# Graph attention with a residual layer norm: seven own blocks for the tile of five to seven keys, one list of edges, and paired small steps in layer norm

## The chip, the core and the metric

The kernel runs on one NeuronCore of a Trainium2 chip. TensorE (PE) multiplies matrices, VectorE (DVE) and ScalarE (ACT) work element by element, GpSimd (POOL) issues the indirect DMAs and computes a few powers, SyncE (SP) issues most plain DMAs. Each engine takes its instructions in the order in which the program wrote them, and waits on semaphores for the others. The metric is the device time of one execution in microseconds (us).

## The reference

`x` is 16 batches of 1024 nodes with 512 features, all in float32. `adj` is a 1024 x 1024 matrix of zeros and ones that all batches share; its chance of a one falls with the row and the column number, so that most nodes have few neighbours and a few have many. There are 8 heads of 64 features.

```python
q = (x @ Wq + bq).reshape(b, n, H, HD)      # k and v likewise
scores = jnp.einsum('bqhd,bkhd->bhqk', q, k) / jnp.sqrt(jnp.float32(HD))
scores = scores + (1.0 - adj)[None, None, :, :] * -1000000000.0
attn = jax.nn.softmax(scores, axis=-1)
out = jnp.einsum('bhqk,bkhd->bqhd', attn, v).reshape(b, n, d)
x = layernorm(x + out @ Wo + bo)            # mean and variance over the 512 features, eps 1e-5
```

A query without any neighbour gives every key the same weight, so its attention is the mean of all values.

## The kernel before

**Tiles and blocks.** The kernel doesn't multiply dense score matrices. It sorts the 1024 nodes by their number of keys (their neighbours) and cuts them into eight tiles of 128 queries: tile 0 has the queries with the fewest keys, tile 7 those with the most. A *block* is 128 pairs of a query and one of its keys. For each block the rows of k and v are gathered from DRAM by an indirect DMA into the tile `kvg` (L1292). There are two kinds of blocks:

- An *own* block of a tile has one key for each of the tile's 128 queries, in the order of the tile. Its queries are the rows of the tile `qt`, loaded once for all own blocks of the tile. A query with fewer keys than the tile has own blocks leaves its place empty: the gather skips it, and a large negative bias takes its weight to zero.
- A *deep* block packs the keys that are left over, of any of the tile's queries. Its queries have to be gathered as well (`qg`, L1246), and its result has to be brought back to the tile's order by a matrix of zeros and ones in `sums`.

`OWN` has the number of own blocks of each tile, `BLOCKS` that of deep blocks, `DEGREE` the length of the list of a query's left-over keys. Before, tile 6 (five to seven keys) had five own blocks and a deep one, and tile 7 seven and five. Tile 1 (one key each) is not computed in blocks at all, and tile 0 is computed for two batches at once from batch 2 on; so a batch has 34 blocks or 32, and the 16 batches have 530.

**What a block costs.** Each block passes these steps: product of q and k on VectorE (`products`, L1313), sum over each head's 64 features on VectorE (`scores`, L1317), exponential on ScalarE (`exponentials`, L1328), and weighing of v by it (`weigh`). The function `by_act` says which engine weighs: own blocks after the first of their tile always go to ScalarE, as eight instructions of one head each (L1341). The first block of a tile and the deep ones go to ScalarE or, as one instruction, to VectorE (L1345), by whether a number is even:

```python
if 0 < i < OWN[t]:
    return True
turn_of = b + i if b and i else n
return n < total - NBT and (turn_of % 2 == 0 or n < NBT // 2)
```

Here `b` is the batch, `i` the block's number in its tile and `n` its number in the whole program. `add_own` adds an own block (but the first) to the tile's first on VectorE (L1357); `add_up` adds a deep block by two products with `sums` on TensorE, which together have four matrix instructions in the trace (L1366, L1367). `normalise` closes a tile: where it had deep blocks, two VectorE instructions add what TensorE has summed (L1378 and L1379), and then each head is divided by its sum.

**Lists of edges.** For a tile with deep blocks `edges(t)` builds the list of left-over keys before they are used: it gathers the tile's rows of `adj`, finds the keys with repeated maxima over 1024 numbers (L646, L665, L667), and places them with small matrix products (L682, L707, L728). `REST_FROM` has the iteration in which each list starts: tile 7 at -24, tile 6 at -6. `ranks` writes the own keys into `key_row` and `absent`, and `lookups` turns each row of keys into places, by one small indirect DMA each.

**The dense part.** `pair`, `transpose_x` and `product` put the work of every batch on TensorE: transposing x, the products with the weights for q, k and v (k and v by a scheme with seven products instead of eight), and the product with `Wo` (`finish`). Until 12 blocks before the last batch starts there is such work ahead in the list `fronts`; after that, only the product with `Wo` is left, some of it from tiles that were spilled to DRAM (`SPILL`).

**The order.** A Python loop writes the whole program, one iteration for each block; it has `n` as its counter. In iteration n it writes the gathers up to block n + 8, the exponential of block n + 3, the product and the sum of block n + 4, the weighing on VectorE of block n + 1 or on ScalarE of block n + 2, and the addition of block n. The function `later(k, ...)` puts an instruction k iterations on, and `later_last` puts it at the end of that iteration. TensorE gets as much dense work in each iteration as `share` and the block's own load allow (`paced`).

**Layer norm.** `complete` adds the residual to a tile (in `Y`, six buffers), and then come a row sum with it on VectorE (L1113), the sum of squares on ScalarE (L1120, `spread`), `variance` on VectorE (L1123), `power` on GpSimd (L1126; L1174 for two tiles), `shift` on VectorE (L1129), `norm_out` on ScalarE (L1134) and the store (L1148). While there is work in `fronts` each tile does all of these by itself (`single`). After that two tiles share the power, and still have a variance and a shift each. `load_y` loads the residual into a buffer of `Y`; it is only called while fewer than five buffers are held.

Of the kernel before, what the change touches and what calls it, by code (L numbers as in the profile page):

```python
# [14 lines left out]
OP = mybir.AluOpType  # L15
# [3 lines left out]
EPS = 1e-5  # L19
# [4 lines left out]

OWN = (2, 1, 2, 3, 4, 5, 5, 7)
BLOCKS = (0, 0, 0, 0, 0, 0, 1, 5)
DEGREE = (8, 8, 8, 8, 8, 8, 16, 80)

AHEAD = 8
KG_BUFS, Q_BUFS, QT_BUFS, PV_BUFS, Y_BUFS = 8, 5, 3, 5, 6
# [29 lines left out]
MORE_RANKS_AT = 1  # L62
NORMS_AT = 18
LOOK_FROM = -17
REST_FROM = {7: -24, 6: -6}

PRODUCT = 0.86
SUM = 0.87
# [6 lines left out]
P = 128  # L75
# [103 lines left out]
def kernel(  # L179
# [36 lines left out]
    nc = tc.nc  # L216
    B, N, D = x.shape
# [5 lines left out]
    scale = 1.0 / HD ** 0.5  # L223
    assert N == 1024 and D == 512 and HD == 64 and max(BLOCKS) <= NT
    NS = sum(BLOCKS)
    NB = NS + sum(OWN)
    first = [sum(BLOCKS[:t]) for t in range(NT)]
    SHORT = [t for t in range(NT) if not BLOCKS[t]]
    SHORT_KEYS = max(OWN[t] for t in SHORT)
    assert SHORT == list(range(len(SHORT))) and max(OWN) <= TOP  # L230
    own = [SHORT_KEYS * t for t in SHORT]
    for t in range(len(SHORT), NT):
        own.append(own[-1] + (OWN[t - 1] if t > len(SHORT) else SHORT_KEYS))
    NK = own[-1] + OWN[-1]
    NBT = NB - OWN[ONE_KEY]
    assert OWN[ONE_KEY] == 1 and BLOCKS[ONE_KEY] == 0

# [17 lines left out]
    with ExitStack() as main:  # L255
# [18 lines left out]
        nc.gpsimd.iota(place, pattern=[[1, SPAN]], base=1, channel_multiplier=0, allow_small_or_imprecise_dtypes=True)  # L274
        placed = one.tile([P, max(BLOCKS)], F32, name="placed")
        nc.gpsimd.iota(placed, pattern=[[P, max(BLOCKS)]], base=1, channel_multiplier=1, allow_small_or_imprecise_dtypes=True)
# [171 lines left out]
        def later(k, fn):  # L448
            plan.setdefault(now[0] + k, []).append(fn)

        def later_last(k, fn):
            rest.setdefault(now[0] + k, []).append(fn)
# [554 lines left out]
        loaded, half, wide = {}, [], []  # L1007
# [89 lines left out]
        def complete(b, t, p, plain):  # L1097
            n, rows, offset = rows_of(b, t)
            y, p = Y[b, t][0:n, :], p[0:n, :]
            ending = not fronts and now[0] >= total - 1  # L1100
            single = fronts or ending or n < P
            if single:
                st = small.tile([P, 5], F32, name="stats", bufs=6)[0:n, :]
            else:

                second = bool(half)
                if not second:
                    half.append([small.tile([P, 2, 5], F32, name="stats_2", bufs=5)])
                st2 = half[0][0]
                st = st2[:, int(second), :]  # L1110
            if plain:
                nc.vector.tensor_tensor(y, p, y, op=OP.add)
            nc.vector.scalar_tensor_tensor(  # L1113
                y, bo_bc[0:n, :] if plain else p, 1.0, y, op0=OP.mult, op1=OP.add, accum_out=st[:, 0:1]
            )

            def spread():

                sq = work.tile([P, D], F32, tag="ysq", name=f"ysq_{b}_{t}", bufs=1)
                nc.scalar.activation(sq[0:n, :], y, AF.Square, bias=st[:, 0:1], scale=-float(D), accum_out=st[:, 2:3])  # L1120

            def variance():
                nc.vector.tensor_scalar(st[:, 2:3], st[:, 2:3], 1.0 / D ** 3, EPS, op0=OP.mult, op1=OP.add)  # L1123

            def power():
                nc.gpsimd.tensor_tensor(st[:, 3:4], st[:, 2:3], neg_half[0:n, :], op=OP.pow)  # L1126

            def shift():
                nc.vector.scalar_tensor_tensor(  # L1129
                    st[:, 4:5], st[:, 0:1], -1.0 / D, st[:, 3:4], op0=OP.mult, op1=OP.mult  # L1130
                )

            def norm_out():
                nc.scalar.activation(y, y, AF.Identity, bias=st[:, 4:5], scale=st[:, 3:4])  # L1134
                if not fronts and now[0] >= total:
                    later_last(1, store)
                else:
                    later(2, store)

            def centre():  # L1140
                nc.vector.tensor_scalar(st[:, 4:5], st[:, 0:1], 1.0 / D, None, op0=OP.mult)

            def last_norm_out():
                nc.vector.tensor_scalar(y, y, st[:, 4:5], st[:, 3:4], op0=OP.subtract, op1=OP.mult)
                store()

            def store():
                nc.gpsimd.indirect_dma_start(  # L1148
                    out=out_rows[b, t], out_offset=bass.IndirectOffsetOnAxis(ap=rows, axis=0),
                    in_=y, in_offset=None, element_offset=offset,  # L1150
                )
                del Y[b, t]

            later_last(0 if ending else 1, spread)
            if ending and (b, t) == closes[total - 1]:
                for step in (centre, variance, power, last_norm_out):
                    later(1, step)
            elif ending:
                later(1, variance)
                later(1, power)  # L1160
                later_last(1, shift)
                later_last(1, norm_out)
            elif single:
                late = 1 if fronts else 0
                later(2 + late, variance)
                later(3 + late, power)
                later(4 + 2 * late, shift)
                later_last(5 + 2 * late, norm_out)
            elif second:
                later(3, variance)  # L1170
                mate_shift, mate_norm_out = half.pop()[1]

                def powers():
                    nc.gpsimd.tensor_tensor(  # L1174
                        st2[:, :, 3:4], st2[:, :, 2:3], neg_half[:, :, None].to_broadcast([P, 2, 1]), op=OP.pow
                    )

                def shifts():
                    mate_shift()
                    shift()  # L1180

                later(4, powers)
                shift_at = 6 if fronts else min(6, max(5, total - now[0]))
                later(shift_at, shifts)
                later_last(shift_at, mate_norm_out)
                later_last(7 if shift_at == 6 else 5, norm_out)
            else:
                later(3, variance)
                mine = half[0]
                mine.append((shift, norm_out))  # L1190

                def alone():
                    if half and half[0] is mine:
                        half.pop()
                        power()
                        later(2, shift)
                        later_last(3, norm_out)

                later(6, alone)

# [281 lines left out]
        done, coming, spilled, gathered, fronts, guarded = [], [], [], [0], [], []  # L1484
# [31 lines left out]
        with tc.manual_schedule():  # L1516
# [20 lines left out]
            n = -LEAD_IN  # L1537
# [120 lines left out]
```

## Time and profile before

| | |
|---|---|
| time, median of 3 runs | 1847.21 us (1845.62 to 1847.8) |
| span of the profiled execution | 1840.4 us |
| median less span | 6.8 us |
| busy, share of the span | PE 98%, DVE 92%, ACT 85%, POOL 66% |
| instructions in the span | 25352 |
| granted TensorE clock, mean | 0.996 |

The profile has one execution, and its own time outside the span is not stated; the median of the runs stands 6.8 us over the span, and differences in the span are carried to the median one for one. "Busy" counts an instruction from its start to its end. Instructions of one engine overlap a little, so what one more of them costs its engine is read from start to start in the timeline, not from its duration. The page that sums up the profile gives, for each group of instructions, the line, the engine, the tiles, the number of instructions after an x, the time busy and the mean of one in ns, and after a bar the idle time ahead of it with what ended it.

### The profile page before, as it was taken

The numbers are of one execution on the slowest core, as the hardware profiler recorded it, in microseconds if no ns is written. First come the engines' busy times: TensorE is split into PE (matmuls) and PEld (weight loads), VectorE is DVE, ScalarE is ACT, GpSimd is POOL, SyncE is SP. The second block draws the span as 40 slices with busy tenths as digits, with TensorE's granted clock in tenths as the row PEclk, the third lists the DMA queues.
The fourth block names the chain that finished last, engine by engine and source line by source line (L and its number), as shares of the span: only waits on it lengthen the run. The fifth ranks groups of instructions, "written<-read, shape, count | busy, mean of one in ns | idle before, by whom it ended". The sixth has DMA issues, their size and how long they took to land.

```text
span 1840.4 us, 25352 instructions
## 1 busy us (share of the span) xinstructions
PE 1798.2 (98%) x5140; PEld 876.2 (48%) x5140; DVE 1693.7 (92%) x3473; ACT 1563.2 (85%) x6183; POOL 1215.3 (66%) x1142
## 2 busy tenths in 40 slices
PE   7999999999999999999999999999999999999997
PEld 3444454554444454444444445444544444444443
DVE  6889889999989999999999999999999999997986
ACT  3637869989889898999889988989799999987886
POOL 1367766766565776767757666677666767665786
PEclk9999999999999999999999999999999999999998
DMA  7358787989889899999988998999989999889995
GB/s 287 106 190 253 256 325 237 346 301 327 308 280 314 295 336 319 344 316 308 347 316 310 346 335 276 343 321 322 339 315 325 314 355 326 306 324 325 338 319 191
DMA packets 198791, 558.54 MB, mean 303 GB/s; under 512 B 33450, under 2 KB 33470, under 8 KB 198626
## 3 DMA queue, kind: packets, MB, share of 16 engines
q0 software_dynamic: 112640, 370.50, 59.3%
q1 hardware_dynamic: 82910, 180.52, 26.2%
q10 hardware_dynamic: 3076, 5.82, 0.9%
q14 instruction: 122, 1.00, 0.2%
q8 instruction: 43, 0.70, 0.2%
HBM read 420.30 MB, written 157.45 MB: 314 GB/s over the span
## 4 chain that ended last, share of the span: by engine, by line
PE 69%; DVE 10%; ACT 9%; DMA 4%; issue 3%; POOL 1%; SPq 0%; POOLq 0%; DVEq 0%; ACTq 0%
PE po L799 17%; PE pq L799 15%; PE pp L956 12%; PE z L956 9%; PE x L956 9%; ACT pv L1341 5%; DVE qk L1313 2%; PE poT L1401 2%; PE pxT L757 2%; PE sum L1367 2%; DVE s L1317 2%; PE sum L1366 2%; DVE pv L1357 1%; ACT sq_k L809 1%; DMA kvg<-kv_pair,place_row 1%
## 5 line engine op out<-in xcount | busy, mean ns | idle before, releaser
L1341 ACT ACTIVATE pv<-kvg,pv 128x64 f32<-128x64 f32 x3600 | 907.5, 341 | 0.0
L1292 POOL DMA_INDIRECT kvg<-kv_pair,place_row x462 | 526.7, 1140 | 307.4 <-ACT pv L1341 99.6
L799 PE MATMUL pq<-wq,xT 128*128 128x512 f32 x792 | 367.8, 596 | 0.0
L1317 DVE TENSOR_REDUCE s<-qk 128x8 f32<-128x512 f32 x530 | 360.7, 681 | 6.8
L799 PE MATMUL po<-wo,oT 128*128 128x512 f32 x792 | 359.3, 594 | 0.7 <-ACT oT L1405 0.7
L1313 DVE TENSOR_TENSOR qk<-qt,kvg 128x512 f32<-128x512 f32 x434 | 297.2, 685 | 1.1 <-DMA kvg<-kv_rows,key_row 0.6
L956 PE MATMUL x<-b,xT 128*128 128x512 f32 x504 | 237.3, 593 | 0.5 <-ACT e L969 0.4
L956 PE MATMUL pp<-t,s 128*128 128x512 f32 x504 | 237.0, 593 | 0.0
L1357 DVE TENSOR_TENSOR pv<-pv,pv 128x520 f32<-128x520 f32 x329 | 228.3, 694 | 4.3 <-ACT pv L1341 4.2
L799 PEld LDWEIGHTS po<-wo,oT 128*128 128x128 f32 x792 | 149.1, 191 | 170.0 <-issue 160.2
L799 PEld LDWEIGHTS pq<-wq,xT 128*128 128x128 f32 x792 | 148.4, 192 | 161.9 <-issue 149.9
L1010 POOL DMA_INDIRECT x<-in_x_dram,asked_row x120 | 133.0, 1108 | 77.8 <-issue 21.3
L1148 POOL DMA_INDIRECT out_dram<-y,asked_row x129 | 146.9, 1139 | 39.1 <-issue 21.2
L1328 ACT ACTIVATE pv<-s,absent 128x8 f32<-128x8 f32 x434 | 127.0, 294 | 44.0 <-DVE s L1317 40.8
L809 ACT ACTIVATE sq_k<-kv 128x128 bf16<-128x128 f32 x512 | 150.8, 301 | 6.4 <-DVE kv L979 3.4
L956 PEld LDWEIGHTS pp<-t,s 128*128 128x128 f32 x504 | 94.7, 191 | 108.1 <-issue 99.4
L956 PEld LDWEIGHTS x<-b,xT 128*128 128x128 f32 x504 | 94.2, 191 | 107.4 <-issue 99.0
L956 PE MATMUL z<-b,s 128*128 128x512 f32 x252 | 119.2, 596 | 7.0 <-DVE kv L984 7.0
L1246 POOL DMA_INDIRECT qg<-q_rows,query_row x96 | 104.4, 1088 | 28.4 <-issue 26.9
L956 PE MATMUL z<-t,s 128*128 128x512 f32 x252 | 118.6, 593 | 0.0
L956 PE MATMUL pp<-t,xT 128*128 128x512 f32 x252 | 118.5, 593 | 0.0
L1134 ACT ACTIVATE y<-y,stats 128x512 f32<-128x512 f32 (+1 forms) x128 | 102.7, 806 | 17.0 <-DVE stats L1129 17.0
(279 smaller groups left out, 2713.0 us busy)
## 6 DMA issues: line engine op xcount, KB each, us to landing
kv_pair<-kv SPq DMA_DIRECT2D x98, 512.0 KB
q_rows<-q SPq DMA_DIRECT2D x106, 256.0 KB
qt<-q_rows SPq DMA_DIRECT2D x98, 256.0 KB
residual<-x SPq DMA_DIRECT2D x83, 256.0 KB
y<-residual SPq DMA_DIRECT2D x83, 256.0 KB
kv_rows<-kv SPq DMA_DIRECT2D x15, 512.0 KB
kvg<-kv_pair,place_row POOLq DMA_INDIRECT x462, 6.9
kv_pair<-kv SPq DMA_DIRECT2D x28, 256.0 KB
```

The source lines that it names most:

```text
L799: nc.tensor.matmul(p, lhs(c), w[:, c, :], start=(c == 0), stop=(c == NPAIR - 1))
L809: nc.scalar.activation(sq, s[:, ts(h, P)], AF.Square, scale=scale, accum_out=sums[:, h:h + 1])
L956: nc.tensor.matmul(R[bank], l[:, ts(c, P)], right[:, c, :], start=(first and c == 0), stop=(c == 1), skip_group_check=True,)
L1010: nc.gpsimd.indirect_dma_start(out=y, out_offset=None, in_=x_rows, in_offset=bass.IndirectOffsetOnAxis(ap=asked_row[:, t:t + 1], axis=0), ...
L1148: nc.gpsimd.indirect_dma_start(out=out_rows[b, t], out_offset=bass.IndirectOffsetOnAxis(ap=rows, axis=0), in_=y, in_offset=None, element_o ...
L1246: nc.gpsimd.indirect_dma_start(out=q, out_offset=None, in_=q_rows[b % ROWS], in_offset=bass.IndirectOffsetOnAxis(ap=rows, axis=0))
L1292: nc.gpsimd.indirect_dma_start(out=KG[n], out_offset=None, in_=rows, in_offset=bass.IndirectOffsetOnAxis(ap=(place_row if b else key_row)[ ...
L1313: nc.vector.tensor_tensor(QK[n], q, KG[n][:, 0:D], op=OP.mult)
L1317: nc.vector.tensor_reduce(S[n], QK.pop(n).rearrange("p (h d) -> p h d", d=HD), axis=AX.X, op=OP.add)
L1328: nc.scalar.activation(PV[n][:, D:], S.pop(n), AF.Exp, bias=bias)
L1341: nc.scalar.activation(pv[:, ts(h, HD)], v[:, ds(D + h * HD, HD)], AF.Copy, scale=pv[:, D + h:D + h + 1])
L1357: nc.vector.tensor_tensor(PV[b, t], PV[b, t], pv, op=OP.add)
```

## The change

Tile 6 gets seven own blocks and no deep one. `SHORT`, the tiles without deep blocks, is then tiles 0 to 6, and the only list of edges that is left is that of tile 7. A batch has 35 blocks or 33, and the program 546, of which 80 are deep where 96 were. Before, tile 6 was the last of each batch from batch 2 on; now its blocks stand ahead of those of tile 7, and tile 7 is the last.

In layer norm the tiles go in pairs also while there is work in `fronts`. A pair has one `variances`, one `powers` and one `shifts`, each for two numbers a row. A tile that finds no second one within nine iterations (five where `fronts` is empty) does the steps alone.

```diff
-OWN = (2, 1, 2, 3, 4, 5, 5, 7)
-BLOCKS = (0, 0, 0, 0, 0, 0, 1, 5)
-DEGREE = (8, 8, 8, 8, 8, 8, 16, 80)
+OWN = (2, 1, 2, 3, 4, 5, 7, 7)
+BLOCKS = (0, 0, 0, 0, 0, 0, 0, 5)
+DEGREE = (8, 8, 8, 8, 8, 8, 8, 80)
...
-REST_FROM = {7: -24, 6: -6}
+REST_FROM = {7: -24}
...
-            single = fronts or ending or n < P
+            single = ending or n < P
...
             elif second:
-                later(3, variance)
-                mate_shift, mate_norm_out = half.pop()[1]
+                mate_norm_out = half.pop()[1]
+
+                def variances():
+                    nc.vector.tensor_scalar(
+                        st2[:, :, 2:3], st2[:, :, 2:3], 1.0 / D ** 3, EPS, op0=OP.mult, op1=OP.add
+                    )
...
                 def shifts():
-                    mate_shift()
-                    shift()
-
+                    nc.vector.scalar_tensor_tensor(
+                        st2[:, :, 4:5], st2[:, :, 0:1], -1.0 / D, st2[:, :, 3:4], op0=OP.mult, op1=OP.mult
+                    )
+
+                later(3, variances)
                 later(4, powers)
                 shift_at = 6 if fronts else min(6, max(5, total - now[0]))
                 later(shift_at, shifts)
                 later_last(shift_at, mate_norm_out)
                 later_last(7 if shift_at == 6 else 5, norm_out)
             else:
-                later(3, variance)
                 mine = half[0]
-                mine.append((shift, norm_out))
+                mine.append(norm_out)
 
                 def alone():
                     if half and half[0] is mine:
                         half.pop()
-                        power()
-                        later(2, shift)
-                        later_last(3, norm_out)
-
-                later(6, alone)
+                        variance()
+                        later(1, power)
+                        later(3, shift)
+                        later_last(4, norm_out)
+
+                later(9 if fronts else 5, alone)
```

## The prediction

> **What bounds the kernel now.** I read the page of the whole span first, then the busy time of each engine in stretches, since a share over the span mixes stages.
>
> ```profile
> span 1840.4 us, 25352 instructions
> ...
> PE 1798.2 (98%) x5140; PEld 876.2 (48%) x5140; DVE 1693.7 (92%) x3473; ACT 1563.2 (85%) x6183; POOL 1215.3 (66%) x1142
> ```
>
> TensorE is busy for nearly the whole span, with VectorE six points behind. The stretches (start and end in us, then length, and busy PE, PEld, DVE, ACT and POOL) show where that holds:
>
> ```profile
> 110.00:300.00 190.00, 184.87 (x534) 88.92 (x534) 167.78 (x367) 139.93 (x577) 135.32 (x127) 1.00 0.79 265
> 300.00:400.00 100.00, 100.00 (x295) 50.06 (x294) 96.72 (x193) 92.38 (x382) 73.21 (x71) 1.00 0.91 324
> 400.00:600.00 200.00, 197.62 (x563) 96.31 (x563) 181.72 (x361) 174.87 (x704) 127.42 (x122) 1.00 0.87 298
> 600.00:700.00 100.00, 100.00 (x290) 49.17 (x290) 97.53 (x194) 90.60 (x360) 74.42 (x67) 1.00 0.93 325
> 700.00:1000.00 300.00, 299.48 (x867) 146.46 (x866) 286.64 (x556) 272.72 (x1127) 199.45 (x179) 1.00 0.92 321
> 1000.00:1100.00 100.00, 96.99 (x283) 47.87 (x282) 96.72 (x186) 89.59 (x364) 68.71 (x65) 1.00 0.96 336
> 1100.00:1200.00 100.00, 100.00 (x295) 49.49 (x294) 94.44 (x186) 91.80 (x379) 62.73 (x58) 1.00 0.89 309
> 1200.00:1300.00 100.00, 99.95 (x289) 49.17 (x288) 97.65 (x193) 94.12 (x381) 72.60 (x65) 1.00 0.92 332
> 1300.00:1400.00 100.00, 99.29 (x293) 49.22 (x292) 95.00 (x183) 89.90 (x375) 66.83 (x61) 1.00 0.91 322
> 1400.00:1500.00 100.00, 99.61 (x289) 48.96 (x287) 97.43 (x193) 93.16 (x368) 70.37 (x66) 1.00 0.92 324
> 1500.00:1600.00 100.00, 95.44 (x278) 46.87 (x277) 98.42 (x190) 94.18 (x403) 65.44 (x60) 1.00 0.94 333
> 1600.00:1841.00 241.00, 225.61 (x620) 107.23 (x618) 199.96 (x494) 188.78 (x648) 166.02 (x157) 0.98 0.83 296
> 1000.00:1025.00 25.00, 25.00 (x74) 12.36 (x73) 24.68 (x51) 23.94 (x99) 17.65 (x18) 1.00 0.94 331
> 1525.00:1550.00 25.00, 22.38 (x63) 10.95 (x62) 24.72 (x47) 23.43 (x95) 18.48 (x18) 1.00 1.00 371
> ```
>
> From 300 to 1400 TensorE hardly pauses and sets the pace. But VectorE has only two to five points of room in most of these stretches, and in 1500:1600 the order is turned round: VectorE at 98.42, TensorE down to 95.44. So two engines share the bound, and the change takes from one of them and gives to the other.
>
> **The deep block, on TensorE.** These rows are the timeline of TensorE (start, length), the two products of one deep block and what follows:
>
> ```profile
> 908.65 0.59 PE L1366 MATMUL sum<-pv,sums 128*128 128x256 f32 x2
> 909.08 0.61 PE L1367 MATMUL sum<-pv,sums 128*128 128x264 f32 x2
> 909.53 1.02 PE L956 MATMUL z<-b,s 128*128 128x512 f32 x2
> ```
>
> From start to start they take 909.53 - 908.65 = 0.88 us. (The durations, 380 and 387 ns a piece, would make 1.53; they overlap, so I take the spacing.) One such block in each of 16 batches goes: 14.1 us.
>
> **The blocks, on VectorE.** The timeline of VectorE, read from start to start in the same way:
>
> ```profile
> 1203.94 0.15 DVE L1378 TENSOR_TENSOR rden<-sum,pv 128x8 f32<-128x8 f32 x1
> 1204.01 0.68 DVE L1379 TENSOR_TENSOR o<-sum,pv 128x512 f32<-128x512 f32 x1
> 1204.61 0.19 DVE L1383 RECIPROCAL rden<-rden 128x8 f32<-128x8 f32 x1
> ...
> 1207.62 0.68 DVE L1313 TENSOR_TENSOR qk<-qt,kvg 128x512 f32<-128x512 f32 x1
> 1208.22 0.69 DVE L1357 TENSOR_TENSOR pv<-pv,pv 128x520 f32<-128x520 f32 x1
> 1208.83 0.68 DVE L1317 TENSOR_REDUCE s<-qk 128x8 f32<-128x512 f32 x1
> 1209.42 0.15 DVE L1129 SCALAR_TENSOR_TENSOR stats<-stats 128x1 f32<-128x1 f32 x1
> 1209.49 0.69 DVE L863 TENSOR_TENSOR vsum<-vsum,kv 128x512 f32<-128x512 f32 x1
> ```
>
> Product 0.60, addition 0.61, sum over heads 0.59, a small step 0.07. A batch gains two own blocks: 2 x 1.80 = +3.60. It loses a deep one: product and sum, -1.19, and L1378 and L1379 in the closing of tile 6, -0.67. That leaves +1.74.
>
> **Who weighs** is less visible. By the rule in `by_act` the first block of a tile goes by whether its number in the program is even. Before, batches have 34 or 32 blocks, so every batch starts at an even number, and in a batch of 34 the first blocks of its tiles stand at 0, 2, 5, 9, 14, 20 and 28: two of seven odd. After, batches have 35 or 33 and every second one starts at an odd number; there the first blocks stand at 0, 2, 4, 8, 13, 19 and 27 from an odd start, which makes four of seven odd. In the other batches (33 blocks) they stand at 0, 2, 6, 11, 17 and 25 from an even start: three odd, where the positions 0, 2, 6, 11, 18 and 26 before had one. With the deep blocks (by b + i) VectorE weighs 6 blocks in every batch from 2 to 14, where it weighed 5 and 4 by turns. Counted over all blocks that is 99 where there were 80.
>
> ```profile
> L1341 ACT ACTIVATE pv<-kvg,pv 128x64 f32<-128x64 f32 x3600 | 907.5, 341 | 0.0
> L1345 DVE TENSOR_TENSOR pv<-kvg,pv 128x512 f32<-128x512 f32 x80 | 54.9, 686 | 0.0
> L1328 ACT ACTIVATE pv<-s,absent 128x8 f32<-128x8 f32 x434 | 127.0, 294 | 44.0 <-DVE s L1317 40.8 <-DVE stats L1123 2.7
> ```
>
> The count of 80 is there. So VectorE has 1.5 more a batch, +0.90 at the 0.60 of like shapes. ScalarE weighs 546 - 99 = 447 blocks for 3600 / 8 = 450: -6 us at 907.5 / 450 = 2.02 each. It has 16 exponentials more, +5. ScalarE stays where it is, and the two extra own blocks of each batch fall on VectorE in the end.
>
> **Layer norm.** The rows before: 97 single powers and 16 for two.
>
> ```profile
> L1126 POOL TENSOR_TENSOR stats<-stats,neg_half 128x1 f32<-128x1 f32 (+1 forms) x97 | 67.2, 693 | 20.7 <-DVE stats L1123 18.9
> ...
> 300.00:1600.00 1300.00, 62.16 (x77) 1.00 0.91 320
> ACT y L1134 <- DVE stats L1129: 17.0, 12, 3.5
> SPq L1035 <- DMA out_dram<-y,asked_row: 36.1, 7, 15.5
> ```
>
> The second row is L1134 alone: 77 tiles are normed between 300 and 1600. Less seven half tiles that stay single and a few without a mate, some 33 pairs each save a variance and a shift: 33 x 2 x 0.07 = 4.6 us, 0.36 a batch. The powers saved lie beside other work on GpSimd, 66% busy. The costs: in a pair the first tile's L1134 now stands in the iteration of the shift, not one later, so ScalarE may wait for VectorE; this is the 17.0 us above, 12 times, all of it after 1700 where pairs exist now. At 17.0 / 16 pairs, 33 pairs would wait 35 us. Queued behind it on ScalarE are the exponential and the weighing of later blocks, which VectorE needs. I cost it at nothing: ScalarE is idle 1300 - 1183 = 117 us from 300 to 1600 (the stretches above). Without that cover it is 35. The first tile of a pair also holds its buffer of `Y` some five iterations longer. SP waits for such a buffer for 36.1 us after 1600 and, in the view of SP's waits, not once between 150 and 1600; behind it stand the stores of q and of k and v. I take nothing here too; if it came here as it does after 1600, it would be some 36.
>
> **Gathers.** 16 more of k and v and 16 fewer of q leave GpSimd's count of issues alone, and no row of k and v is added, as empty places are skipped.
>
> **The list of tile 6.**
>
> ```profile
> L665 DVE MAX8 kl<-codes 128x8 f32<-128x1024 f32 x2 | 2.4, 1217 | 0.0
> PE z L956 <- DVE kv L984: 1.1, 1, 1.1
> ```
>
> Two maxima of 1.2 us over 1024 numbers, two more passes over as many and a dozen small steps leave VectorE. TensorE loses only what waited: 1.1 us between 110 and 150 (second row), and about 0.5 of small products. I take -1.6; the bounds are 0 and TensorE's whole idle time in 110:300, 5.1.
>
> **The sum, stretch by stretch.** Sums over heads (L1317) count the blocks:
>
> ```profile
> 110.00:300.00 190.00, 30.30 (x45) 1.00 0.79 265
> 300.00:1600.00 1300.00, 288.90 (x425) 1.00 0.91 320
> 1600.00:1841.00 241.00, 41.48 (x61) 0.98 0.83 296
> ```
>
> At 530 / 16 = 33.1 to a batch that is 1.36, 12.8 and 1.84 batches, so nearly one in each 100 us between 300 and 1600. There TensorE loses 0.88 per 100 us, and VectorE gains 1.74 + 0.90 - 0.36 = 2.28. A stretch then takes the longer of two times: TensorE's new busy time with the idle time that it has now, or VectorE's new busy time divided by the share that it can reach. That share is the unknown: 0.984 was reached over 100 us (1500:1600), 0.987 to 0.989 over 25 us (the last two rows of the stretches), 0.9695 over 1300 to 1600 ((95.00 + 97.43 + 98.42) / 300). I take 0.984, from the only stretch in which VectorE plainly led:
>
> - 300: (96.72 + 2.28) / 0.984 = 100.6, so +0.6; in the same way 600: +1.4, 1000: +0.6, 1200: +1.6, 1400: +1.3, 1500: +2.3. Sum +7.8.
> - 400 to 600 stays TensorE's: -1.8; 1100 and 1300 too: -0.9 each. 700 to 1000: VectorE has 293.5 / 0.984 = 298.3, so -1.7. Sum -5.3.
>
> That is +2.5 from 300 to 1600. Elsewhere TensorE leads: 1.36 x 0.88 = -1.2 and -1.6 for the list before 300, 1.84 x 0.88 = -1.6 after 1600. Total -1.9 on a span of 1840.4; taken off the median of 1847.2 (6.8 above the span), about 1845. At 0.988 the stretches give -0.9 and the time is 1842, and at 0.980 they give +6.5 and 1849. In own blocks the addition stands between the product and the sum that needs it, as in the rows above, which should fill VectorE a little better than deep blocks do; so I take **1844**.
>
> The Trainium skill speaks against the change here. Its page "Perfetto Trace Analysis", section "Identifying the Most-Contended Engine", says that matmul busy time is no good measure for TensorE, that its weight loads are (48% here), and that occupancy is fair for VectorE. VectorE with 92% would then be the engine to relieve, and the sum would be its growth alone, 1876 (the last rival), in place of 1844. The trace agrees in 1500:1600 and not in 300:400, where TensorE has no gap.
>
> **The rivals.**
>
> - *TensorE keeps the end throughout.* VectorE reaches 0.99 and more and its extra work fits: -0.88 x 12.8 - 4.4 = -15.7, so 1831.5. For it: 1000:1025, with TensorE at 25.00 and VectorE at 24.68. Against: 1525:1550, where VectorE at 24.72 left TensorE at 22.38.
> - *VectorE takes over and can't be filled better than over 1300 to 1600*, 0.9695. Each stretch with VectorE over 95% now then grows: 300 +2.1, 600 +2.9, 700 to 1000 +2.7, 1000 +2.1, 1200 +3.1, 1400 +2.8, 1500 +3.9, less 1.7 in the others: +17.9, with -4.4 outside +13.5, so **1861**, slower. It decides from a share of about 0.98 downward. For it: the dense work comes to VectorE in lumps. Against: the share rose in the stretches when there was more to do.
> - *The pairs bring waits*: of the 35 us on ScalarE a third reaches VectorE, 1844 + 12 = 1856. Against it is ScalarE's 117 us of idle time.
> - *VectorE bounds all of the span as it is.* Then its growth, 12.8 x 2.28 = 29, is added in full: 1876. Against it: in 1100:1200 VectorE has 94.44 and TensorE no gap at all. The rule of the Trainium skill named above would have it so.
>
> **How the numbers follow.** Forecast 0.45 (its own range 1840 to 1850), TensorE throughout 0.27, VectorE at the lower share 0.17, waits by pairs 0.06, VectorE everywhere 0.05. A measurement of this kernel tells about 0.2%, 3.7 us, from no change. Faster by more: 0.27 and a good third of the forecast, 0.43. Slower: most of the last three, 0.25. The rest, 0.32, is within. The range of 1830 to 1858 leaves out the far ends of the first and the slower rivals.
>
> **What would show it.** After, L1366 and L1367 should have 160 each, L1345 99 and L1341 3576, and powers for two should be near 50. VectorE should stand at 97 to 98.5% in most stretches from 300 to 1600, with TensorE at 97 to 99. TensorE above 99% throughout would speak for the first rival, VectorE at 97 or less with TensorE at 97 or less for the second, and L1134 waiting for L1129 before 1600 for the third. The prediction is wrong if VectorE's busy sum doesn't rise by 20 to 35 us.

## The result and the profile after

The changed kernel takes 1878.27 us (1873.15 to 1879.64) where the kernel before takes 1847.21: 1.016 times as long, interval 1.0146 to 1.0174. That is slower, 34 us over the forecast of 1844 and 20 over the end of the range.

The page of the changed kernel: span and busy time.

```profile
span 1877.9 us, 25037 instructions
...
PE 1803.6 (96%) x5071; PEld 864.8 (46%) x5071; DVE 1717.2 (91%) x3387; ACT 1566.2 (83%) x6174; POOL 1216.1 (65%) x1102
```

VectorE has 23.5 us more to do than before and ScalarE 3.0. TensorE is the surprise: on each of the two lines of a deep block it has 160 instructions where it had 192, some 14 us less in all, yet its busy time *rose* by 5.4 us. Its idle time, span less busy, went from 42.2 us to 74.3. So the 37.5 us of span are 32.1 of new idle time on TensorE and 5.4 of longer busy time.

Groups of the changed kernel (line, operation, count, then busy us and mean ns); each form came in the number that the prediction gives, or near it:

```profile
L1323 DVE TENSOR_REDUCE s<-qk 128x8 f32<-128x512 f32 x546 | 371.1, 680 | 6.1
L1351 DVE TENSOR_TENSOR pv<-kvg,pv 128x512 f32<-128x512 f32 x99 | 67.8, 685 | 0.0
L1347 ACT ACTIVATE pv<-kvg,pv 128x64 f32<-128x64 f32 x3576 | 900.6, 339 | 0.0
L1178 POOL TENSOR_TENSOR stats<-stats,neg_half 128x2 f32<-128x2 f32 x56 | 45.4, 811 | 20.2 <-DVE stats L1173 18.1 <-ACT pv L1334 0.2
L1372 PE MATMUL sum<-pv,sums 128*128 128x256 f32 x160 | 49.1, 389 | 4.4 <-DVE pv L1351 3.9 <-ACT pv L1347 0.4
```

Stretches of the changed kernel (length, then busy PE, PEld, DVE, ACT, POOL; PEclk is the third number from the end):

```profile
300.00:400.00 100.00, 95.40 (x268) 47.30 (x267) 92.40 (x176) 89.92 (x369) 69.83 (x64) 0.97 0.86 302
400.00:600.00 200.00, 200.00 (x575) 97.02 (x574) 191.10 (x365) 176.90 (x717) 136.72 (x118) 1.00 0.88 305
...
700.00:1000.00 300.00, 292.49 (x840) 141.17 (x839) 287.80 (x544) 270.99 (x1106) 195.22 (x173) 1.00 0.90 313
...
1200.00:1300.00 100.00, 93.55 (x263) 44.35 (x262) 95.49 (x182) 89.48 (x361) 66.39 (x58) 1.00 0.88 303
1300.00:1400.00 100.00, 97.25 (x281) 47.24 (x282) 94.91 (x181) 86.89 (x362) 64.12 (x59) 1.00 0.91 319
1400.00:1500.00 100.00, 96.54 (x271) 45.97 (x270) 94.42 (x180) 86.68 (x345) 58.25 (x53) 0.98 0.85 289
1500.00:1600.00 100.00, 93.77 (x262) 44.50 (x262) 95.35 (x177) 87.03 (x360) 66.51 (x59) 0.98 0.91 321
```

Look for an engine without gaps: from 1200 to 1600 there is none, with TensorE at 94 to 97 and VectorE at 94 to 95. Where TensorE had 299.48 of 300 us (700:1000) it has 292.49. VectorE's share is lower than before in 1400:1600, though it has more to do. The chain that ended last, of the kernel before and then of the changed one, says the same:

```profile
PE 69%; DVE 10%; ACT 9%; DMA 4%; issue 3%; POOL 1%; SPq 0%; POOLq 0%; DVEq 0%; ACTq 0%
```

```profile
DVE 24%; PE 21%; ACT 21%; issue 8%; DMA 8%; POOL 3%; POOLq 0%; SPq 0%; DVEq 0%; ACTq 0%
```

A chain that ran along TensorE now hops between three engines. Waits (total us, times, longest), first one of the kernel before, then those of the changed one:

```profile
ACT pv L1328 <- DVE s L1317: 41.5, 40, 2.7
```

```profile
ACT pv L1334 <- DVE s L1323: 101.0, 85, 5.0
...
ACT y L1134 <- DVE stats L1183: 30.8, 18, 5.1
...
POOL kvg L1298 <- DMA kv_pair<-mean: 8.3, 1, 8.3
```

ScalarE's exponential waits for VectorE's sum for 101.0 us (41.5 before), and one gather waits 8.3 us for the row with the mean of v, the last row of k and v that a batch needs before its blocks can start. The kernel before has no such wait.

**Where in the program the time goes.** The first sum over heads of a batch marks its start; batches are counted from 0. The table has that start, less that of the kernel before, in us; "last" is the last such sum. Runs of the experiments below stand beside it.

| | batch 2 | 4 | 10 | 12 | 14 | last | end |
|---|---|---|---|---|---|---|---|
| changed | +1.5 | -5.3 | -1.0 | +7.6 | +25.4 | +32.5 | +37.5 |
| e1, blocks only | +2.7 | -3.2 | +1.3 | +7.0 | +24.3 | +32.2 | +34.6 |
| e2, norms only | -1.4 | -1.8 | -2.1 | -2.7 | -0.8 | +5.6 | +9.5 |
| f1, changed, EARLY 17 | +9.2 | +5.9 | +12.0 | +15.0 | +29.6 | +35.9 | +37.8 |
| g1, before, VectorE +29 | +3.9 | +5.8 | +16.1 | +18.5 | +23.2 | +23.1 | +23.2 |
| g2, changed, VectorE -32 | +1.9 | -6.7 | -6.9 | 0.0 | +15.4 | +19.4 | +24.4 |

The changed kernel is not behind at all at batch 10, and loses 26 us in the four batches after that. What had happened before shows in the number of dense products on TensorE (L799 and L956) between these marks: from the start of batch 0 to the end of batch 5 there are 1328 in the kernel before and 1311 in the changed one; in batch 13 it is 174 and 191. So the changed kernel put 17 products off and did them in batch 13. This is the batch in both profiles, before and then after:

```profile
1493.90:1587.60 93.70, 89.14 (x269) 44.49 (x268) 92.20 (x176) 87.47 (x367) 62.71 (x57) 1.00 0.94 334
```

```profile
1507.00:1613.00 106.00, 99.10 (x282) 47.10 (x280) 96.29 (x180) 92.34 (x385) 68.49 (x61) 0.98 0.88 315
```

It takes 12.3 us longer, 10.0 of them in TensorE's busy time. A start that is "on time" at batch 10 hides a debt: at 0.43 us a product (four from start to start take 1.72), 17 make 7 us. But the debt alone doesn't make this batch long. In f1, described below, nothing is put off and the batch has 179 products; it still takes 104.5 us, with more idle time on TensorE:

```profile
1512.80:1617.30 104.50, 95.28 (x269) 45.85 (x269) 95.88 (x179) 90.18 (x380) 63.35 (x57) 0.97 0.87 295
```

### The profile page after: what moved, and what is told of

Its sections match the earlier page's. It is cut to its first block, busy times and chain, and to the rows that moved or that the text cites. A ratio compares the mean times of both kernels' runs of the same rounds, so it can differ in the third digit from the quotient of the medians.

```text
span 1877.9 us, 25037 instructions
## 1 busy us (share of the span) xinstructions
PE 1803.6 (96%) x5071; PEld 864.8 (46%) x5071; DVE 1717.2 (91%) x3387; ACT 1566.2 (83%) x6174; POOL 1216.1 (65%) x1102
## 4 chain that ended last, share of the span: by engine, by line
DVE 24%; PE 21%; ACT 21%; issue 8%; DMA 8%; POOL 3%; POOLq 0%; SPq 0%; DVEq 0%; ACTq 0%
ACT pv L1347 13%; PE po L799 7%; DVE qk L1319 5%; DVE s L1323 4%; DMA kvg<-kv_pair,place_row 4%; PE pp L956 3%; PE pq L799 3%; DVE pv L1363 2%; PE x L956 2%; PE z L956 2%; ACT sq_k L809 2%; ACT y L1134 1%; DVE y L1112 1%; ACT pv L1334 1%; DVE q L830 1%
## 5 line engine op out<-in xcount | busy, mean ns | idle before, releaser
L1298 POOL DMA_INDIRECT kvg<-kv_pair,place_row x476 | 558.4, 1173 | 315.2 <-ACT pv L1347 88.8
L1323 DVE TENSOR_REDUCE s<-qk 128x8 f32<-128x512 f32 x546 | 371.1, 680 | 6.1
L799 PE MATMUL pq<-wq,xT 128*128 128x512 f32 x792 | 366.2, 595 | 0.0
L799 PE MATMUL po<-wo,oT 128*128 128x512 f32 x792 | 362.5, 593 | 1.4 <-ACT oT L1411 0.7
L1319 DVE TENSOR_TENSOR qk<-qt,kvg 128x512 f32<-128x512 f32 x466 | 318.6, 684 | 15.7 <-DMA kvg<-kv_pair,place_row 10.7
L1363 DVE TENSOR_TENSOR pv<-pv,pv 128x520 f32<-128x520 f32 x361 | 250.4, 694 | 9.8 <-ACT pv L1347 9.6
L956 PE MATMUL x<-b,xT 128*128 128x512 f32 x504 | 239.3, 597 | 5.1 <-ACT e L969 5.1
L956 PE MATMUL pp<-t,s 128*128 128x512 f32 x504 | 238.3, 595 | 0.3 <-DVE t L384 0.3
L799 PEld LDWEIGHTS po<-wo,oT 128*128 128x128 f32 x792 | 147.5, 190 | 171.2 <-issue 158.1
L799 PEld LDWEIGHTS pq<-wq,xT 128*128 128x128 f32 x792 | 148.2, 191 | 165.2 <-issue 153.4
L1334 ACT ACTIVATE pv<-s,absent 128x8 f32<-128x8 f32 x466 | 136.1, 294 | 82.4 <-DVE s L1323 74.7
L1148 POOL DMA_INDIRECT out_dram<-y,asked_row x129 | 151.9, 1177 | 44.7 <-issue 19.0
L956 PEld LDWEIGHTS x<-b,xT 128*128 128x128 f32 x504 | 94.8, 190 | 117.3 <-issue 102.9
L956 PEld LDWEIGHTS pp<-t,s 128*128 128x128 f32 x504 | 94.7, 191 | 114.5 <-issue 105.8
L1134 ACT ACTIVATE y<-y,stats 128x512 f32<-128x512 f32 (+1 forms) x128 | 103.1, 807 | 35.9 <-DVE stats L1183 30.8
L956 PE MATMUL pp<-t,xT 128*128 128x512 f32 x252 | 120.4, 600 | 6.2 <-DVE y L1112 3.9
L956 PE MATMUL z<-b,s 128*128 128x512 f32 x252 | 119.3, 595 | 6.0 <-DVE kv L984 6.0
L956 PE MATMUL z<-t,s 128*128 128x512 f32 x252 | 120.8, 602 | 0.0
L1252 POOL DMA_INDIRECT qg<-q_rows,query_row x80 | 88.4, 1104 | 23.6 <-issue 18.7
```

The costliest lines, as they stand in the source:

```text
L799: nc.tensor.matmul(p, lhs(c), w[:, c, :], start=(c == 0), stop=(c == NPAIR - 1))
L956: nc.tensor.matmul(R[bank], l[:, ts(c, P)], right[:, c, :], start=(first and c == 0), stop=(c == 1), skip_group_check=True,)
L1148: nc.gpsimd.indirect_dma_start(out=out_rows[b, t], out_offset=bass.IndirectOffsetOnAxis(ap=rows, axis=0), in_=y, in_offset=None, element_o ...
L1298: nc.gpsimd.indirect_dma_start(out=KG[n], out_offset=None, in_=rows, in_offset=bass.IndirectOffsetOnAxis(ap=(place_row if b else key_row)[ ...
L1319: nc.vector.tensor_tensor(QK[n], q, KG[n][:, 0:D], op=OP.mult)
L1323: nc.vector.tensor_reduce(S[n], QK.pop(n).rearrange("p (h d) -> p h d", d=HD), axis=AX.X, op=OP.add)
```

## The experiments

Four theories stood at first: **V**, VectorE's added work sets the time; **N**, the pairs of layer norm make ScalarE wait; **L**, the dense work loses its lead over the blocks; **Y**, a pair holds its buffer of `Y` too long. Later **T** (TensorE and its pauses), **C** (three engines near their bounds, each one's work counts in part), **R** (ScalarE is full in the long run of own blocks of tiles 6 and 7) and **S** (V's work early and the dense work that slipped, paid late) came in. All ratios are to the kernel before, on the same chip.

**e1, the blocks alone.** The constants of the change, layer norm as before.

```diff
+OWN = (2, 1, 2, 3, 4, 5, 7, 7)
+BLOCKS = (0, 0, 0, 0, 0, 0, 0, 5)
+DEGREE = (8, 8, 8, 8, 8, 8, 8, 80)
+REST_FROM = {7: -24}
```

> The blocks alone: tile 6 with seven own blocks and one list of edges, layer norm as before. Theory V (VectorE's added work sets the time): VectorE has all of the change's added work and not the 0.36 us a batch that the pairs save, so the time stands at or a few us above the changed kernel, 1876 to 1884. Theory N (the pairs of layer norm, which make ScalarE wait for VectorE's shift, cost the time): without them ScalarE's wait for the shift before 1600 us is gone and the time is back at 1842 to 1852.

**e2, layer norm alone.** The rest of the change, the constants as before.

> The pairs of layer norm alone, with the blocks and lists of before. Theory V: VectorE loses some 4 us of small steps, so the time is 1842 to 1848, the same as before or a little less. Theory N: ScalarE's wait of some 30 us for the shift shows and the time is 1865 to 1880.

e1: 1870.93 us, 1.0126 (1.0108 to 1.0145). e2: 1855.23 us, 1.005 (1.0035 to 1.0065). The blocks make some 23 us of the loss and the pairs some 9, together about the whole; added to the blocks, the pairs make 6 (1.0160 less 1.0126). The table shows that e2 has lost nothing at the start of batch 14, and at that of batch 15 it is 4.4 us ahead. GpSimd in e2, late in batch 15:

```profile
1787.45 0.94 POOL L1038 DMA_INDIRECT y<-in_x_dram,asked_row  x1 [3.38 <-DMA out_dram<-y,asked_row]
1788.69 1.70 POOL L1252 DMA_INDIRECT qg<-q_rows,query_row  x1 [0.31 <-issue]
1790.69 1.02 POOL L1298 DMA_INDIRECT kvg<-kv_pair,place_row  x1 [0.30 <-DMA y<-in_x_dram,asked_row]
```

A load of `Y` waits for a store to free its buffer, and the last three gathers of the last batch stand behind it in GpSimd's queue. In the kernel before, the load of `Y` that comes there is issued behind the last gather, at 1794.20 (the gather at 1791.02). And in e2's waits TensorE stands 8.9 us for a tile of the output, the longest such wait of that kernel:

```profile
PE poT L1407 <- DVE o L1393: 11.5, 2, 8.9
```

**f2, layer norm alone, pairs stopped before the end.** No new pair is begun while fewer than 40 pieces of dense work are left.

```diff
-            single = ending or n < P
+            single = ending or n < P or 0 < len(fronts) < 40 and not half
```

> The pairs of layer norm alone (blocks as before), but with single tiles again as soon as fewer than 40 units of dense work are left and no tile waits for a mate, so that the stage after 1690 us is written just as before the change. Theory Y (a tile that waits for its mate holds a buffer of Y into the last stage, delays a tile there by an iteration, and all behind it): the 9 us of the pairs alone are gone, 1841 to 1848. If the pairs cost by their steps themselves (ScalarE's wait for the shift), the time stays at 1852 to 1857.

1846.71 us, 0.9999 (0.9985 to 1.0014): all of the 9 us are back, with 52 pairs still made. The price of the pairs is thus not in the pairs but in the passage to the last stage, as theory Y has it: in f2 the last load of `Y` is again issued behind the last gather and waits 0.3 us. That the buffer is the whole of the 9 us is read from the order and not shown by a run that frees the buffer alone. In the changed kernel the wait is not there (its last two loads of `Y` wait 0.3 us each), while f4 below, which has f2's edit, has one of 2.9 us; so how the pairs cost time there stays open. In f2 they bring nothing either: VectorE has 5.8 us less to do than before (1687.9 for 1693.7) and the time is the same.

**e4, the first tile of a pair normed one iteration later.**

```diff
-                later_last(shift_at, mate_norm_out)
-                later_last(7 if shift_at == 6 else 5, norm_out)
+                later_last(7 if fronts else shift_at, mate_norm_out)
+                later_last((8 if fronts else 7) if shift_at == 6 else 5, norm_out)
```

> The changed kernel with both normalising steps of a pair one iteration later while there is dense work ahead, so that ScalarE doesn't come to the first of them in the iteration of the shift. Theory V: no change, 1875 to 1881. Theory N: ScalarE's 30.8 us of waiting for the shift shrink to 5 to 15 and the time falls by 10 to 25 us.

1879.54 us, 1.0182 (1.0156 to 1.0208). The wait did shrink:

```profile
ACT y L1134 <- DVE stats L1183: 13.9, 8, 3.9
```

From 30.8 to 13.9, and the time did not follow. f2 keeps 22.1 us of the same wait and loses nothing. Theory N falls; these waits are covered, as the prediction took it.

**e3, fewer weighs on VectorE.** The turn goes by tile and not by the number in the program, 79 weighs on VectorE for 99.

```diff
-            turn_of = b + i if b and i else n
+            turn_of = b + i if i else int(t in (3, 7))
```

> The changed kernel with one rule exchanged: the first blocks of tiles 3 and 7 are weighed by VectorE and those of the other tiles by ScalarE, so that VectorE weighs 79 blocks, as before (80), and not 99. Theory V: VectorE's busy sum falls by 12 us, and the time by as much or a little more, to 1862 to 1868, though ScalarE gets 20 x 2.02 = 40 us more. Theory N: the time hardly moves, 1874 to 1880, or rises with ScalarE's load.

1878.19 us, 1.0173 (1.0149 to 1.0197). VectorE had 9.8 us less and ScalarE some 37 more (1603.5 busy); nothing gained. It speaks against VectorE as the only bound, but two engines were changed at once, so it does not settle it.

**f1, the changed kernel with more lead for the dense work; f3, the kernel before with less (EARLY 11); f4, the changed kernel with EARLY 17 and the edits of f2 and e4.** The edit of f1:

```diff
-EARLY = 13
+EARLY = 17
```

> The changed kernel with EARLY at 17 and not 13, so that the dense work of a batch is written further ahead of its first block: the rows of k and v of the last batches are then complete 10 to 12 blocks ahead, and not 6 to 8. Theory L (the change eats up the lead of the dense work, and late batches wait for the rows that they gather): the 25 us lost between the starts of batches 11 and 14 are mostly regained, 1850 to 1862. Theory V (VectorE's added work sets the time everywhere): no change, 1874 to 1881.

> The kernel before, with EARLY at 11 and not 13 and nothing else: its last batches then have leads of 7 to 9 blocks where they had 9 to 10. Theory L: the same kind of loss shows without any of the change, 1852 to 1870, with waits for gathered rows near the starts of batches 13 and 14. Theory V: no change, 1843 to 1850.

> The changed kernel with EARLY at 17, with single tiles once fewer than 40 units of dense work are left, and with both normalising steps of a pair one iteration later. Theory L with Y: all of what was lost is regained and some of TensorE's 14 us of saved work shows, 1832 to 1846. Theory V: 1868 to 1880.

f1: 1880.31 us, 1.0171 (1.0136 to 1.0206). f3: 1851.99 us, 1.0023 (1.0004 to 1.0042). f4: 1876.87 us, 1.0145 (1.0105 to 1.0186). With EARLY 17 no products are put off (1334 by the end of batch 5, 179 in batch 13) and the gather's wait of 8.3 us is gone, but the table shows 9 us lost by batch 2 and 12 by batch 10. Lead by itself is neither the cause nor the cure: from batch 10 to 14 the loss is 17.6 us in place of 26.4, and the difference is lost earlier. f3, with less lead, loses 4 us: the lead counts, but for little. f4 isn't told from the changed kernel.

**g1 to g4, one engine loaded or relieved at a time.** g1, the kernel before with three products of tile 7 made twice in each batch; g3, with four copies of the transposed output made twice on ScalarE; g4, with the two products of the first deep block of tiles 6 and 7 made twice; g2, the changed kernel without three of seven additions to the sum of v. The edits of g1, g2, g3 and g4:

```diff
+            for again in range(2 if b and t == NT - 1 and 0 < i < 4 else 1):
+                nc.vector.tensor_tensor(QK[n], q, KG[n][:, 0:D], op=OP.mult)
...
-                    for v in kv:
+                    for v in kv[:1]:
                         nc.vector.tensor_tensor(VSUM[b], VSUM[b], v, op=OP.add)
...
+                    for again in range(2 if b and 2 <= t < 6 else 1):
+                        nc.scalar.copy(OT[b, t], p)
...
+            if b and i == 0:
+                nc.tensor.matmul(PSUM[b, t][:, 0, 0:HD2], m, pv[:, 0:HD2], start=True, stop=True)
+                nc.tensor.matmul(PSUM[b, t][:, 1, 0:HD2 + HEADS], m, pv[:, HD2:], start=True, stop=True)
```

> The kernel before, in which VectorE makes the products of three blocks of tile 7 of each batch from the second on twice: 45 products of 0.68 us with some 0.07 us between two starts, 34 us more for VectorE and nothing for another engine (the result is the same). Theory V (VectorE's work sets the time between its waits, some 150 us of which it keeps in both kernels): 1875 to 1882 us, as slow as the changed kernel. Theory T (TensorE sets it, and only its pauses cost): the 34 us lie in VectorE's 153 us of idle time, 1846 to 1854. Theory C (three engines are near their bound and each one's added work costs a part): 1856 to 1870.

> The changed kernel with three of the seven additions for the sum of v of each batch left out (the mean of v is wrong by that): 48 additions of 0.69 us, 36 us less for VectorE with the time between starts, nothing for another engine. Theory V: back to 1840 to 1850 us. Theory T: 1870 to 1878, since TensorE's and ScalarE's work is what it was. Theory C: 1856 to 1868.

> The kernel before, in which ScalarE makes the copies of the transposed output of tiles 2 to 5 twice in each batch from the second on: 60 copies of 0.575 us, 38 us more for ScalarE with the time between starts (the result is the same). Theory V: ScalarE has some 280 us idle, 1846 to 1852 us. Theory T: the same. Theory C: 1854 to 1866.

> The kernel before, in which TensorE makes the two products of the first deep block of tiles 6 and 7 twice in each batch from the second on: 60 products, 0.88 us a block, 26 us more for TensorE alone (the result is the same). Theory V: TensorE's work fills pauses only in part, 1848 to 1856 us. Theory T: 1868 to 1874, all of it is seen. Theory C: 1854 to 1866.

The pages of g1, g3, g4 and g2:

```profile
PE 1805.4 (97%) x5127; PEld 875.7 (47%) x5140; DVE 1722.9 (92%) x3518; ACT 1568.4 (84%) x6183; POOL 1227.4 (66%) x1142
```

```profile
PE 1804.6 (97%) x5127; PEld 875.7 (47%) x5140; DVE 1694.2 (91%) x3473; ACT 1598.4 (86%) x6243; POOL 1230.8 (66%) x1142
```

```profile
PE 1824.4 (98%) x5247; PEld 897.2 (48%) x5260; DVE 1695.1 (91%) x3473; ACT 1566.7 (84%) x6183; POOL 1227.2 (66%) x1142
```

```profile
PE 1798.0 (96%) x5057; PEld 864.8 (46%) x5071; DVE 1685.7 (90%) x3339; ACT 1567.4 (84%) x6174; POOL 1225.3 (66%) x1102
```

| | busy time added | time | ratio (interval) | seen per us added |
|---|---|---|---|---|
| g1 | VectorE +29.2 | 1864.62 | 1.0094 (1.0067 to 1.0121) | 17.4 / 29.2 = 0.6 |
| g3 | ScalarE +35.2 | 1857.84 | 1.0050 (1.0033 to 1.0067) | 9.2 / 35.2 = 0.26 |
| g4 | TensorE +26.2 | 1869.60 | 1.0117 (1.0099 to 1.0135) | 21.6 / 26.2 = 0.8 |
| g2 | VectorE -31.5, to the changed kernel | 1867.14 | 1.0096 (1.0062 to 1.0130) | (1.0160 - 1.0096) x 1847 = 11.8; 0.4 |

("Seen" is ratio less one, by 1847.) Theory C stands, against V and T as the only cause: a us on any of the three engines is seen in part, and the shares add up to more than one. No engine "has the bound"; each pauses because of the others.

**h1 to h4 and i1, i2, work and order in the changed kernel.** h1, g2's additions left out and EARLY 17; h2, tile 6 behind tile 2; h3, VectorE weighs the own blocks 4 of tile 6 and 3 of tile 7 and leaves the first blocks of tiles 0 to 4 to ScalarE; h4, the own blocks 5 and 6 of tile 6 weighed in one ScalarE instruction, with the first head's weight for all heads; i1, e1 with h2's order; i2, e1 again beside it.

The edit of h2 and i1, then of h3, then of h4:

```diff
+            tiles.sort(key=lambda t: 2.5 if t == 6 else t)
```

```diff
+            if 0 < b < B - 1 and 0 < i < OWN[t]:
+                return (t, i) not in ((6, 4), (7, 3))
+            if b and i == 0 and t < 5 and n < total - NBT:
+                return True
```

```diff
+            if b and t == 6 and i > 4:
+                nc.scalar.activation(pv[:, 0:D], v[:, D:], AF.Copy, scale=pv[:, D:D + 1])
+                return
```

> The changed kernel with both taken away at once: 48 of the additions for the sum of v left out (the mean of v is wrong by that; VectorE 36 us less) and EARLY 17 for 13 (the dense work keeps its lead of some 9 blocks through the last batches). Alone the first gave 1867 us and the second 1880. Theory S (VectorE's added work is paid early and the dense work that slipped is paid late, so that each alone only moves the loss): 1842 to 1856. Theory R (ScalarE is full in the long run of own blocks of tiles 6 and 7, whatever VectorE and the lead do): 1862 to 1870.

> The changed kernel with the blocks of tile 6 behind those of tile 2 in every batch from the third on, so that no run of 13 own blocks with their seven weighs each on ScalarE is left at the end of a batch; all work is the same. Theory R: 1860 to 1870, since ScalarE's 6 to 12 us of idle time in the first half of a batch are used. Theory S: no change, 1874 to 1880.

> The changed kernel with VectorE's weighs at other places: in batches 1 to 14 it weighs the own blocks 4 of tile 6 and 3 of tile 7 and leaves the first blocks of tiles 0 to 4 to ScalarE; its weighs are 100 in all, 99 before. Theory R: ScalarE is relieved by 2 x 1.9 us a batch where it has no idle time, 1862 to 1872. Theory S: VectorE's work is the same, 1874 to 1882.

> The changed kernel in which ScalarE weighs the own blocks 5 and 6 of tile 6 of batches 1 to 15 in one instruction for all heads (with the first head's weight, which is not what is to be computed), some 0.6 us in place of 1.93 us: 40 us less for ScalarE in the run of own blocks, nothing else. Theory R: 1850 to 1864. Theory S: ScalarE's work counts little, 1870 to 1878.

> The two own blocks of tile 6 alone, layer norm as before, and tile 6 behind tile 2 in the order of the blocks of every batch from the third on. Theory R (ScalarE is full in the run of 13 own blocks of tiles 6 and 7): ratio to the kernel before 1.002 to 1.007, against some 1.013 with the order as it was. Theory C (three engines within 5 per cent of their bounds, in changing places; the order moves the place only): 1.010 to 1.014.

> The two own blocks of tile 6 alone once more, as the measure for the run beside it on the same chip: by all theories the ratio to the kernel before that it had, 1.011 to 1.0145.

These two sets ran on two chips on which the kernel before itself took 1866.6 and 1872.69 us; there the profiles stand 8 to 28 us behind by batch 1 already, so only ratios are read. h1: 1.0063 (1.0037 to 1.0089). h2: 1.0105 (1.0048 to 1.0162). h3: 1.0128 (1.0065 to 1.0190). h4: 1.0100 (1.0070 to 1.0130). i1: 1.0084 (1.0062 to 1.0106), and i2 beside it 1.0115 (1.0092 to 1.0139).

- h1 leaves 12 us of the changed kernel's 30. The pairs are still in it; alone they cost 9, beside the blocks 6. Its time, some 1859 on the chip of the other runs, is just over theory S's 1842 to 1856. What EARLY 17 could not do alone (f1) and less work for VectorE only in part (g2), the two may do together; the margin over g2 lies within the intervals, so it isn't shown. The reason would be that dense work needs VectorE too and can be early only where VectorE has room.
- h4 takes 35.5 us from ScalarE and is 1.0100: about 11 us seen, 0.3 per us, as in g3 and no more. Theory R asked for 14 to 28. h3, which moves 28 of ScalarE's blocks out of that run and leaves the sums as they were, can't be told from the changed kernel.
- The order of tile 6 (h2, i1) may bring some 6 us: i1 is 1.0084 and i2 1.0115, with intervals that overlap. 1.0084 lies between R's 1.002 to 1.007 and C's 1.010 to 1.014. It stays open.

No version with the two own blocks beat the kernel before, and f2 equals it.

## Why the prediction was wrong

**The counts and prices held.** 160 instructions on each line of deep blocks, 99 weighs on VectorE, 3576 instructions of weighing on ScalarE and 56 pairs came as worked out; ScalarE stayed flat (+3.0 us), and VectorE rose by 23.5 us, inside the 20 to 35 by which the prediction wanted to be judged.

**The step that failed is the sum:** "A stretch then takes the longer of two times: TensorE's new busy time with the idle time that it has now, or VectorE's new busy time divided by the share that it can reach." It has two faults.

- *TensorE does not keep "the idle time that it has now".* In the changed kernel it pauses 74.3 us for 42.2, and it isn't any one wait: the pauses are spread over batches 4 to 14, at 0.2 to 6.9 us a batch, where the kernel before has 0 to 4.6; these eleven batches make some 27 of the 32.1 us. The runs g1 and g3 contradict a longer-of-two rule: it has no term for ScalarE, whose 35 us in g3 cost 9; and it would have charged g1, which loads VectorE as the change does and saves nothing on TensorE, about the +7.8 of the stretches where VectorE leads, and g1 cost 17.4. With 97% on one engine and 95% on the next, work on either is seen.
- *The saving on TensorE was taken as won.* Its 14.1 us were saved, but its busy time rose. The granted clock is why for the most part: 0.996 before and 0.989 after, which is 0.004 x 1840 = 7 us against 0.011 x 1878 = 21 us. (Some 4 us of each fall after TensorE's last product, where it has nothing to do.) Pauses bring the lower clock (last section).

With the measured shares the change would cost 0.6 x 23.5 - 0.8 x 14.1 = +3 us in place of the 20 to 23 that the blocks cost. So sizes and shares alone do not explain it either, and what makes up the rest stays open. The products put off to batch 13 (7 us) and the wait for the row of the mean (8.3 us, on one gather) were found, but f1 has neither and is no faster; h1, where both are gone and VectorE is relieved, has 12 us left with the pairs in it. Not told apart is also how much is the order of tile 6, which the prediction did not cost at all though the diff moves it ahead of tile 7, and why batches 12 and 13 together still take 11.6 us longer in h1 than in the kernel before.

**"I take nothing here too; if it came here as it does after 1600, it would be some 36":** the pairs alone cost 9 us (e2, f2), in the tail and not in the stretches where the price was sought; a hold of `Y` is seen there. The place was named, with the wrong time for it. **"I cost it at nothing"** for ScalarE's wait for the shift was right: the wait grew from 17.0 to 30.8, and halving it (e4) brought nothing.

**The list of tile 6** is not told apart: batch 1 starts 0.9 us earlier, the right sign, against -1.6 for the list and -1.2 for TensorE's saving.

**The rivals.** TensorE throughout (1831.5) fell. VectorE at the lower share (1861) had the right mark from 1200 to 1600, both engines at 97 or less, and the right sign, but its price was short by 17 us; 6.1 of them (1.7 + 4.4) are the saving that it let TensorE keep. VectorE everywhere gave 1876, near the time that was measured; its mechanism is not what the runs show. By it the nine batches before batch 10 would have cost 9 x 2.28 = 20 us, and batch 10 starts 1.0 us early, or 6 late with the 17 products that it still owes; and g1's steady load is seen at 0.6 and not in full. The Trainium skill's page "Perfetto Trace Analysis", section "Identifying the Most-Contended Engine", pointed to VectorE by occupancy; the direction was right here. But relieving VectorE by 31.5 us (g2) gave only 11.8, so the trace does not bear out that one engine is to be optimized first.

## What to carry to other kernels

Where two or three engines stand above 85 to 98% of the same stretches, don't take the longer of two sums: price a us on each by its own measured share, reckon with new pauses that eat a saving on the leader, and test the sum by a run: here it gave 3 us of some 20. Read progress in every kind of work, not only in the visible one: a batch that starts on time may have put its dense products off. And look for the price of a buffer that is held longer where its queue changes stage, not on average.

## What the hardware showed that was not expected

Short pauses of TensorE can bring its granted clock to one half for some 3.4 us afterwards. Stretches of the changed kernel, a pause, what follows it, and the time after that; then a second pause:

```profile
1612.30:1616.20 3.90, 0.04 (x2) 0.01 (x1) 3.87 (x9) 3.21 (x17) 3.29 (x3) 1.00 1.03 417
1616.50:1619.90 3.40, 3.40 (x6) 1.28 (x5) 3.40 (x8) 3.36 (x13) 2.48 (x4) 0.50 0.97 347
1619.90:1623.30 3.40, 3.40 (x12) 1.73 (x11) 3.37 (x8) 2.69 (x10) 2.79 (x3) 1.00 0.87 283
...
1487.70:1489.50 1.80, 0.00 (x0) 0.00 (x0) 1.80 (x5) 1.80 (x10) 0.54 (x1) 1.00 0.83 295
1490.20:1493.50 3.30, 3.30 (x6) 1.22 (x5) 3.23 (x7) 0.93 (x3) 0.00 (x0) 0.50 0.84 340
```

Six products after the pause, twelve in as long a time after that. A pause of 2 us was enough once, while in the kernel before one of 3.0 us had no effect:

```profile
1062.90:1065.80 2.90, 0.00 (x0) 0.00 (x0) 2.51 (x7) 2.90 (x12) 2.40 (x4) 1.00 0.76 232
1065.90:1072.70 6.80, 6.80 (x18) 3.51 (x19) 5.39 (x10) 3.77 (x16) 5.17 (x6) 1.00 0.94 315
```

So the length of a pause does not decide alone; what else does, no run here shows. A kernel that pauses more often pays twice, once for the pause and now and then half of 3.4 us, 1.7, for the clock. The Trainium skill's page "TensorE: Matmul & The Clock Gate", section "Part 1: The HAM clock gate", has the half rate after an idle window of some 3.4 us, with a window that runs freely; the length of the half-rate time agrees, and the pauses that brought it here were in part shorter.
